# Gate exponentials in one batch, the layer norm on ScalarE in place, and another SyncE order in the setup of a Mamba-times-MoE layer

## The chip, the cores and the metric

The kernel runs on one core of a Trainium2 chip. The metric is the device time of one execution in microseconds (us), lower is better. The time before is the median of three runs. One more execution was recorded by the hardware profiler, and every duration below is from that record, counted from its first instruction.

## The reference

Everything is float32. The input x has 2 sequences of 2048 tokens of 256 channels, 4096 tokens in all. It is normalised, goes through a Mamba mixer with an MLP (s) and through a mixture of experts (g), and the two results are multiplied.

```python
xn = layernorm(x)
s = xn + mamba_mixer(rmsnorm(xn))        # d_inner 512, d_state 16, conv of 4, scan over 2048 steps
s = s + silu(rmsnorm(s) @ mlp_w1.T) @ mlp_w2.T
p = softmax(xn @ gate_w + gate_b)        # 8 experts
pk, ek = top_k(p, 2)
g = silu(sum_k pk * (relu(xn @ w1[ek] + b1[ek]) @ w2[ek] + b2[ek]))
out = x + s * g
```

The mixer's scan is h = h * exp(dt * A) + dt * u * B, y = sum over states of h * C, where dt, B and C come from projections of the convolved input.

## The kernel before, in words

The instructions of each engine run in the order in which the program writes them; nothing is reordered by a planner. A small class `Later` delays some instructions by a number of ticks, and `tick()` advances it; generators such as `front(c)` yield "wait" to ask for a tick. So the order of work between the stages is fixed when the program is built.

The tokens stand in eight blocks of 512 (NBLK), each as four rows-of-128 tiles (J). The kernel has two stages.

**The setup** runs over the blocks. `load_x` brings block b into the buffer with tag `B{b}`. `moments(b)` takes mean and variance on VectorE (DVE). `factors` turns them into scales (a logarithm and an exponential on ScalarE, ACT, and a Newton step on DVE). `norm(b)` writes the doubly normalised rows `xr` on ACT (L254) and transposes them on TensorE (PE, L265) into PSUM. `logits(b)` makes the layer-normed rows `xn` in a buffer of its own, tag `C{b}`: two of the four tiles on DVE (L275), two on ACT (L280). It stores them to DRAM (`xnd`, L284), copies the transposed rows out of PSUM into `xrT[b]`, in the buffer `B{b}` that held x (L288), stores these too (`xrd`), and computes the gate logits with small matmuls (L293) into one PSUM bank, `bank_y`.

Every two blocks (GB) make a group of eight tiles, for which `gate(g)` runs on DVE (L378 to L423): the top two experts of each token, a count of the tokens per expert through two matmuls (L394, L397), and from it the row (`slot`) to which each token goes. `gate(g)` also exponentiates the logits on ACT (L417, L419) and computes the two probabilities from them (L420 to L423). `scatter(g)` then issues 16 indirect DMAs on GpSimd (POOL, L435), each of which writes 128 rows of `xn` to their slots in the DRAM tensor `xs_d`; after each stands a memset of one column named `turn` (L442). Between the groups, `forward(3)` runs three ticks of `front(0)`, the projections and convolution of the first block of the scan.

After the fourth group `tiles_of_experts` (L445 to L504) works out which expert each of 39 tiles of 256 rows belongs to. SyncE (SP) then issues, in this order: the weights of the first expert tile (8 loads of 256 KB, L767 and L774), zeros for the unfilled ends of the tiles (`fill_up`, 8 stores, L510), and the first tile's rows `xs` (`rows()`, L892). SP reads the expert numbers and slots out of SBUF as register values before it issues.

`front(0)` continues: `project_x` writes the scan's B and C for the block to the DRAM tensor `bcd` (L580), and `exp_v` and `log_v` make dt (L598 to L617). They use buffers of the tag `yk`, of which there are two; the tile `zeros` holds one of them in the setup. From the first wait after `project_x` on, `draw` also emits expert work. An expert tile is `transpose` (L799), matmuls with w1 (L809), relu (L909), matmuls with w2 (L821), with the next tile's loads in between. Only when `front(0)` has ended are B and C loaded for all eight pairs of states, each 512 KB broadcast to 128 partitions (`load_bc`, L666), into the buffers `B{g}` and `C{g}`.

**The main loop** has 256 steps (block c, channel group d, pair of states g). A step multiplies by B on DVE (L1260), scans on DVE (L1264), multiplies by C on POOL (L1185), and accumulates on PE (L1157). Beside it `draw` emits the expert tiles, later the MLP tiles, so that PE is kept busy.

Of the kernel before, what the change touches and what calls it, by code (L numbers as in the profile page):

```python
# [22 lines left out]
J = T // P  # L23
# [3 lines left out]
NI = NT // P  # L27
TS = 256
JS = TS // P
# [4 lines left out]
NSLOT = NE * CAP  # L34
GB = 2
GI = GB * T // P
# [13 lines left out]
def kernel(  # L50
# [18 lines left out]
    nc = tc.nc  # L69
# [149 lines left out]

    stat = rows.tile([P, 8, NI], F32, tag="x1", name="stat")  # L220
    mv = stat[:, 0:2, :].rearrange("p a i -> p (a i)").rearrange("p (i a) -> p i a", a=2)
    xns, pts = [], {}

    def moments(b):
        st = hpool.tile([P, J, nc.vector.BN_STATS_DIM], F32, tag="hid", name=f"st{b}")
        for j in range(J):
# [39 lines left out]
        pts[b] = pt  # L266

    def logits(b):
        pool, tag = (bcp, f"B{b}") if b else (rows, "xrT")
        xt = xts[b]  # L270
        xn = bcp.tile([P, J, DM], F32, tag=f"C{b}", name=f"xn{b}")
        for j in range(J):
            i = b * J + j
            if j < 2:
                nc.vector.tensor_scalar(  # L275
                    xn[:, j, :], xt[:, j, :], mv[:, i, 0:1], rstd[:, i : i + 1],
                    ALU.subtract, ALU.mult,
                )
            else:
                nc.scalar.activation(  # L280
                    xn[:, j, :], xt[:, j, :], AF.Identity,
                    scale=rstd[:, i : i + 1], bias=moff[:, i : i + 1],
                )
        nc.sync.dma_start(xnd[b], xn)  # L284
        xns.append(xn)
        xrT[b] = pool.tile([P, KM, T], F32, tag=tag, name=f"xrT{b}")
        for k in range(KM):
            nc.scalar.copy(xrT[b][:, k, :], pts[b][k])  # L288
        if b > 0:
            nc.sync.dma_start(xrd[b], xrT[b])  # L290
        for j in range(J):
            for k in range(KM):
                nc.tensor.matmul(  # L293
                    lgp[:, b * J + j, :], xrT[b][:, k, ts(j, P)], gw_sb[:, k, :],
                    start=(k == 0), stop=(k == KM - 1),
                )


    class Later:
# [63 lines left out]
    halves = [rows.tile([P, 5, GI * NE], F32, tag="ys", name=f"halves{k}") for k in range(2)]  # L363
    scratch = rows.tile([P, JS * DM], F32, tag="x1", name="scratch")
    slots = scratch[:, JS * DM - TOPK * NI :].rearrange("p (k i) -> p k i", k=TOPK)

    def gate(g):
        i = slice(g * GI, (g + 1) * GI)
        sh = [P, GI, NE]
        big = [halves[k][:, n, :] for k in range(2) for n in range(5)]  # L370
        sel = [big[n].rearrange("p (i e) -> p i e", e=NE) for n in range(TOPK)]
        lg, left = (big[n].rearrange("p (i e) -> p i e", e=NE) for n in (2, 3))
        mask, tot_e, ahead = (big[n].rearrange("p (e i) -> p e i", e=NE) for n in (4, 5, 6))
        pr = big[7].rearrange("p (i e) -> p i e", e=NE)
        top = [scratch[:, k * GI : (k + 1) * GI] for k in range(TOPK)]
        first, tot = (scratch[:, k * GI : (k + 1) * GI] for k in range(TOPK, TOPK + 2))
        vec = nc.vector
        vec.tensor_tensor(  # L378
            lg, lgp[:, i, :], unr[:, i].unsqueeze(2).to_broadcast(sh), ALU.mult
        )  # L380
# [12 lines left out]
        flat = [P, NE * GI]  # L393
        nc.tensor.matmul(  # L394
            counts[:, 0, :], all1, mask.rearrange("p e i -> p (e i)"), start=True, stop=True
        )
        nc.tensor.matmul(  # L397
            counts[:, 1, :], earlier, mask.rearrange("p e i -> p (e i)"), start=True, stop=True
        )
        vec.tensor_tensor(pr, lg, top[0].unsqueeze(2).to_broadcast(sh), ALU.subtract)  # L400
        vec.tensor_copy(tot_e, counts[:, 0, :].rearrange("p (e i) -> p e i", e=NE))

        vec.tensor_tensor_scan(
            ahead.rearrange("p e i -> p (e i)"), same.rearrange("p e i -> p (e i)"),
            tot_e.rearrange("p e i -> p (e i)"), 0.0, ALU.mult, ALU.add,
        )
        vec.tensor_sub(tot_e, ahead, tot_e)
        vec.tensor_add(tot_e, tot_e, counts[:, 1, :].rearrange("p (e i) -> p e i", e=NE))
        vec.tensor_tensor(
            tot_e, tot_e, ends[:, 0, :].unsqueeze(2).to_broadcast([P, NE, GI]), ALU.add  # L410
        )
        for k in range(TOPK):
            vec.tensor_mul(sel[k], sel[k], tot_e.rearrange("p e i -> p i e"))  # L413
            vec.tensor_reduce(slots[:, k, i], sel[k], AX.X, ALU.add)
            vec.tensor_copy(slot[:, k, i], slots[:, k, i])
        vec.tensor_add(ends[:, 0, :], ends[:, 0, :], ahead[:, :, GI - 1])
        nc.scalar.activation(pr, pr, AF.Exp)  # L417
        vec.tensor_sub(top[1], top[1], top[0])
        nc.scalar.activation(top[1], top[1], AF.Exp)  # L419
        vec.tensor_reduce(tot, pr, AX.X, ALU.add)  # L420
        vec.tensor_single_scalar(tot, tot, 2.0, ALU.mult)
        vec.reciprocal(prob[:, 0, i], tot)
        vec.tensor_mul(prob[:, 1, i], top[1], prob[:, 0, i])  # L423

    turn = small.tile([P, 1], F32, tag="turn", name="turn", bufs=1)

    def to_slots(ins):

        tc.declare_no_dep(ins, group="to_slots", reason="other rows")
        tc.add_to_no_dep_group("to_slots", ins)  # L430

    def scatter(g):
        for i in range(g * GI, (g + 1) * GI):
            for k in range(TOPK):
                r = nc.gpsimd.indirect_dma_start(  # L435
                    out=xs_d,
                    out_offset=bass.IndirectOffsetOnAxis(ap=slot[:, k, i : i + 1], axis=0),
                    in_=xns[i // J][:, i % J, :],
                    in_offset=None,
                )  # L440
                to_slots(r.ins)
                nc.gpsimd.memset(turn, 0.0)  # L442


    def tiles_of_experts():  # L445
# [214 lines left out]
    def load_bc(c, g, which_ones="BC"):  # L660
        later.free("bcd", c)
        for which in which_ones:
            i = "BC".index(which)
            t = bcp.tile([P, 2, T], F32, tag=f"{which}{g}", name=f"{which}{c}_{g}")
            r = i * DS + 2 * g
            nc.sync.dma_start(  # L666
                t, bcd[c][r : r + 2, :].unsqueeze(0).to_broadcast([P, 2, T])
            )
            bct[c, which, g] = t
# [383 lines left out]
    def tick():  # L1053
        later.now += 1
        later.run()
# [10 lines left out]
        logits(b)  # L1066
    factors(GB, NBLK)
    gate(0)
    scatter(0)
    ffns = [Expert(i) for i in range(NTILE)] + [  # L1070
        Mlp(c, hf) for c in range(NBLK) for hf in range(2)
    ]
# [2 lines left out]
    def forward(ticks):  # L1075

        for got in first:
            if got == "wait":
                tick()
                ticks -= 1  # L1080
                if not ticks:
                    return

    for b in range(GB, NBLK + 1):
        if b < NBLK:
            norm(b)
        if b > GB:
            logits(b - 1)
        if b > GB and b % GB == 0:
            gate(b // GB - 1)  # L1090
            scatter(b // GB - 1)
            forward(3)
    tiles_of_experts()
    xrT[1] = rows.tile([P, KM, T], F32, tag="xrT", name="xrTr1")
    nc.sync.dma_start(xrT[1], xrd[1])
    ffns[0].begin()
# [1 line left out]
        ffns[0].load_w1(h)  # L1098
        ffns[0].load_w2(h)
    fill_up()  # L1100
    for _ in ffns[0].rows():
        pass

    hs, ys, y_n, hts, das, dus = {}, {}, {}, {}, {}, {}

# [113 lines left out]
    for got in first:  # L1219
        if got == "wait":  # L1220
            tick()
            if 0 in bcd:
                draw(HALF)
    tick()
    for which in "BC":
        for g in range(DS // 2):
            load_bc(0, g, which)
    for _ in range(LEAD):
        tick()
        draw(HALF)  # L1230
# [118 lines left out]
```

## Time and profile before

| | us |
|---|---|
| median of 3 runs (lowest to highest) | 1624.94 (1622.39 to 1628.21) |
| the profiled execution, its own time | 1645.22 |
| span of the profiled execution, first to last instruction | 1643.2 |
| PE busy in the span | 1412.1 (86%) |
| DVE busy | 1287.7 (78%) |
| POOL busy | 1130.7 (69%) |
| ACT busy | 863.7 (53%) |
| first, second, third and fourth start of L378 (a gate) | 32.10, 62.66, 92.88, 123.03 |
| end of the last scatter instruction | 150.6 |
| first step of the scan (L1264) | 195.9 |

Busy time is what an engine spends in instructions. A line such as "DVE h L1264" means engine, tile written, line of the program. In a timeline the columns are start, duration, engine, line, operation, what is written and read, how many instructions are merged, and in brackets the idle time of the engine just before with what ended it. "SPq" is a DMA issue of SyncE. The profiled execution is 20.3 us longer than the median of the runs shown.

### The profile page before, as it was taken

The numbers are of one execution on the slowest core, as the hardware profiler recorded it, in microseconds if no ns is written. First come the engines' busy times: TensorE is split into PE (matmuls) and PEld (weight loads), VectorE is DVE, ScalarE is ACT, GpSimd is POOL, SyncE is SP. The second block draws the span as 40 slices with busy tenths as digits, with TensorE's granted clock in tenths as the row PEclk, the third lists the DMA queues.
The fourth block names the chain that finished last, engine by engine and source line by source line (L and its number), as shares of the span: only waits on it lengthen the run. The fifth ranks groups of instructions, "written<-read, shape, count | busy, mean of one in ns | idle before, by whom it ended". The sixth has DMA issues, their size and how long they took to land. (4 is left out here: it accounts for less than half of the span.)

```text
span 1643.2 us, 18570 instructions
## 1 busy us (share of the span) xinstructions
PE 1412.1 (86%) x5278; PEld 989.7 (60%) x5278; DVE 1287.7 (78%) x1452; ACT 863.7 (53%) x1832; POOL 1130.7 (69%) x809
## 2 busy tenths in 40 slices
PE   2543769999899999998999999999889879799967
PEld 2430537677567766675677666756566556567736
DVE  7234457877997899869988998798699978899952
ACT  3421644655566556544765565556645555555513
POOL 1654034667688868986898689868885587878842
PEclk7655879999999999999999999999999989899978
DMA  5444544349244924582358245833582336735322
GB/s 184 152 168 143 210 162 132 100 142 345 65 130 156 325 81 124 154 311 87 111 185 315 77 127 175 296 100 104 189 312 72 103 103 210 259 114 167 115 90 83
DMA packets 203718, 266.22 MB, mean 162 GB/s; under 512 B 21713, under 2 KB 174161, under 8 KB 203617
## 3 DMA queue, kind: packets, MB, share of 16 engines
q1 hardware_dynamic: 197472, 248.26, 45.7%
q0 software_dynamic: 6144, 16.79, 3.1%
q8 instruction: 42, 0.69, 0.2%
q14 instruction: 60, 0.48, 0.1%
HBM read 228.02 MB, written 36.96 MB: 161 GB/s over the span
## 5 line engine op out<-in xcount | busy, mean ns | idle before, releaser
L1185 POOL TENSOR_TENSOR h<-h,C 128x1024 f32<-128x1024 f32 x256 | 609.0, 2381 | 321.5 <-ACT hs L1181 201.2
L1264 DVE TENSOR_TENSOR_SCAN h<-da,hs,b 128x512 f32<-128x512 f32 x384 | 481.3, 1272 | 27.5 <-PE y L1157 4.6
L1144 ACT ACTIVATE da<-dt,a_neg 128x512 f32<-128x512 f32 x512 | 357.2, 718 | 36.9 <-DVE h L1264 36.8
L1157 PE MATMUL y<-h,ident 128*128 128x512 f32 x626 | 315.1, 608 | 24.5 <-POOL h L1187 22.4
L1260 DVE TENSOR_TENSOR b<-du,B 128x1024 f32<-128x1024 f32 x256 | 314.7, 1229 | 7.8 <-DMA B<-bcd 1.9
L809 PE MATMUL phe<-xsTe,w_e 128*128 128x256 f32 x1248 | 292.1, 385 | 9.3 <-ACT hide L909 4.0
L821 PE MATMUL poe<-w_e,hide 128*128 128x256 f32 x1248 | 289.3, 381 | 0.0
L809 PEld LDWEIGHTS phe<-xsTe,w_e 128*128 128x128 f32 x1248 | 239.7, 193 | 78.7 <-issue 29.8
L821 PEld LDWEIGHTS poe<-w_e,hide 128*128 128x128 f32 x1248 | 236.5, 191 | 64.6 <-issue 32.4
L1187 POOL TENSOR_TENSOR h<-h 128x512 f32<-128x512 f32 x199 | 257.9, 1296 | 15.6
L909 ACT ACTIVATE hide<-phe,b 128x256 f32<-128x256 f32 x312 | 129.7, 468 | 143.0 <-PE phe L809 143.0
L1157 PEld LDWEIGHTS y<-h,ident 128*128 128x128 f32 x626 | 116.8, 193 | 117.4 <-issue 66.4
L1264 DVE TENSOR_TENSOR_SCAN h<-da,b 128x512 f32<-128x512 f32 x128 | 152.0, 1212 | 15.3 <-PE y L1157 6.5
L809 PE MATMUL phm<-xsTm,w_m 128*128 128x256 f32 x512 | 125.6, 399 | 22.6 <-DVE hidm L970 17.4
L809 PEld LDWEIGHTS phm<-xsTm,w_m 128*128 128x128 f32 x512 | 101.8, 201 | 51.8 <-DVE hidm L970 20.3
L821 PE MATMUL pom<-w_m,hidm 128*128 128x256 f32 x512 | 122.2, 389 | 2.5 <-DVE xom L1041 1.7
L821 PEld LDWEIGHTS pom<-w_m,hidm 128*128 128x128 f32 x512 | 99.3, 196 | 29.4 <-issue 13.3
L435 POOL DMA_INDIRECT xs_d<-xn,slot x64 | 62.3, 973 | 73.3 <-DVE halves L413 61.9
L997 POOL DMA_INDIRECT ykm<-ys_d,row_y x64 | 61.4, 960 | 36.3 <-issue 12.2
L552 DVE SCALAR_TENSOR_TENSOR xc<-px,par_sb,xc 128x512 f32<-128x512 f32 x96 | 71.6, 746 | 13.0 <-ACT xc L544 10.6
L968 ACT ACTIVATE hidm<-phm 128x512 f32<-128x512 f32 x64 | 37.5, 590 | 77.0 <-PE phm L809 76.6
L921 DVE TENSOR_TENSOR ys<-poe,b 128x512 f32<-128x512 f32 x39 | 26.6, 681 | 50.9 <-PE poe L821 48.6
(175 smaller groups left out, 1433.1 us busy)
## 6 DMA issues: line engine op xcount, KB each, us to landing
w_e<-in_w SPq DMA_DIRECT2D x312, 256.0 KB
B<-bcd SPq DMA_DIRECT2D x64, 512.0 KB
C<-bcd SPq DMA_DIRECT2D x64, 512.0 KB
w_m<-in_mlp_w1T SPq DMA_DIRECT2D x64, 256.0 KB
w_m<-in_mlp_w2T SPq DMA_DIRECT2D x64, 256.0 KB
xs<-xs_d SPq DMA_DIRECT2D x39, 256.0 KB
ys_d<-ys SPq DMA_DIRECT2D x39, 256.0 KB
b<-in_b SPq DMA_DIRECT2D x39, 128.0 KB
```

Of the source, the lines that this page charges most:

```text
L435: r = nc.gpsimd.indirect_dma_start(out=xs_d, out_offset=bass.IndirectOffsetOnAxis(ap=slot[:, k, i : i + 1], axis=0), in_=xns[i // J][:, i ...
L552: nc.vector.scalar_tensor_tensor(v[:, s : s + T], px, conv_w[:, d, KC - 1 - s : KC - s], v[:, s : s + T], ALU.mult, ALU.add,)
L809: nc.tensor.matmul(ph[:, q, :], self.w1[c0 // 2][:, k, ts(q, P)], self.xT[:, k, :], start=(k == 0), stop=(k == KM - 1),)
L821: nc.tensor.matmul(po[:, j, :], self.hid[c // 2][:, c % 2, ts(j, P)], self.w2[c // 2][:, c % 2, :], start=(c == 0 and j == 0), stop=(c == ...
L909: nc.scalar.activation(hc[:, q, :], ph[:, q, :], AF.Relu, bias=self.b1[:, c0 + q : c0 + q + 1])
L997: nc.gpsimd.indirect_dma_start(out=yk[k][:, j, :], out_offset=None, in_=ys_d, in_offset=bass.IndirectOffsetOnAxis(ap=row_y[:, k, i0 + j : ...
L1144: nc.scalar.activation(das[n][:, q, :], dts[c, d], AF.Exp, scale=a_neg[:, d, 2 * g + q : 2 * g + q + 1])
L1157: nc.tensor.matmul(ys[c, d], ident, hts[n][:, q, :], start=False, stop=(g == DS // 2 - 1 and q == nq - 1),)
L1185: nc.gpsimd.tensor_tensor(hts[n], hts[n], bct[c, "C", g], ALU.mult)
L1187: nc.gpsimd.tensor_tensor(hts[n][:, 0, :], hts[n][:, 0, :], hts[n][:, 1, :], ALU.add)
L1260: nc.vector.tensor_tensor(inp, dus[c, d].unsqueeze(1).to_broadcast([P, 2, T]), bct[c, "B", g], ALU.mult,)
L1264: nc.vector.tensor_tensor_scan(hts[n][:, q, :], das[n][:, q, :], inp[:, q, :], 0.0 if c % CPB == 0 else hs[c - 1][:, d, 2 * g + q : 2 * g ...
```

## The change

The exponentials leave the gate. Each `gate(g)` writes its shifted logits into a part of one tile for all groups, `exps_of` (tag `yk`), and the difference of the two top logits into `behind`. A new function `probabilities()`, called once after `tiles_of_experts`, does the two exponentials and the four DVE operations for all 32 tiles together.

The layer norm is done by ACT alone, for all four tiles of a block, in place in the buffer of x, and after the copies and logits matmuls instead of before them. `xrT[b]` goes to the buffer `C{b}`. So `B{b}` is now the buffer from which rows are scattered.

The scatter loses the memset and has a bounds check. `front(0)` gets one tick after every block from the fourth on, six in all, instead of three ticks after every second block, nine in all.

In SP's order the loads of B and C, and the first tile's rows, move: at the first wait after `project_x`, six loads of B, eight of C, the first tile's rows, and the last two of B are issued, ahead of the second tile's weights. The zeros stay behind the first tile's weights.

```diff
     def logits(b):
-        pool, tag = (bcp, f"B{b}") if b else (rows, "xrT")
-        xt = xts[b]
-        xn = bcp.tile([P, J, DM], F32, tag=f"C{b}", name=f"xn{b}")
-        for j in range(J):
-            ...
-            if j < 2:
-                nc.vector.tensor_scalar(xn[:, j, :], xt[:, j, :], mv[...], rstd[...], ...)
-            else:
-                nc.scalar.activation(xn[:, j, :], xt[:, j, :], AF.Identity, ...)
-        nc.sync.dma_start(xnd[b], xn)
-        xns.append(xn)
+        pool, tag = (bcp, f"C{b}") if b else (rows, "xrT")
         xrT[b] = pool.tile([P, KM, T], F32, tag=tag, name=f"xrT{b}")
         ...
+        xn = xts[b]
+        for j in range(J):
+            i = b * J + j
+            nc.scalar.activation(
+                xn[:, j, :], xn[:, j, :], AF.Identity,
+                scale=rstd[:, i : i + 1], bias=moff[:, i : i + 1],
+            )
+        nc.sync.dma_start(xnd[b], xn)
...
+    behind = scratch[:, JS * DM - (TOPK + 1) * NI : JS * DM - TOPK * NI]
+    exps_of = rows.tile([P, NI, NE], F32, tag="yk", name="exps_of")
     def gate(g):
...
-        pr = big[7].rearrange("p (i e) -> p i e", e=NE)
+        pr = exps_of[:, i, :]
...
-        nc.scalar.activation(pr, pr, AF.Exp)
-        vec.tensor_sub(top[1], top[1], top[0])
-        nc.scalar.activation(top[1], top[1], AF.Exp)
-        vec.tensor_reduce(tot, pr, AX.X, ALU.add)
-        vec.tensor_single_scalar(tot, tot, 2.0, ALU.mult)
-        vec.reciprocal(prob[:, 0, i], tot)
-        vec.tensor_mul(prob[:, 1, i], top[1], prob[:, 0, i])
+        vec.tensor_sub(behind[:, i], top[1], top[0])
+
+    def probabilities():
+        nc.scalar.activation(exps_of, exps_of, AF.Exp)
+        nc.scalar.activation(behind, behind, AF.Exp)
+        tot = scratch[:, 0:NI]
+        nc.vector.tensor_reduce(tot, exps_of, AX.X, ALU.add)
+        nc.vector.tensor_single_scalar(tot, tot, 2.0, ALU.mult)
+        nc.vector.reciprocal(prob[:, 0, :], tot)
+        nc.vector.tensor_mul(prob[:, 1, :], behind, prob[:, 0, :])
...
-    def scatter(g):
+    def scatter(i, k):
+        r = nc.gpsimd.indirect_dma_start(
+            out=xs_d,
+            ...
+            in_=xts[i // J][:, i % J, :],
+            in_offset=None,
+            bounds_check=NSLOT - 1,
+            oob_is_err=False,
+        )
+        to_slots(r.ins)
+
+    def scatter_group(g):
         for i in range(g * GI, (g + 1) * GI):
             for k in range(TOPK):
-                r = nc.gpsimd.indirect_dma_start(out=xs_d, ..., in_=xns[i // J][:, i % J, :], in_offset=None)
-                to_slots(r.ins)
-                nc.gpsimd.memset(turn, 0.0)
+                scatter(i, k)
...
             gate(b // GB - 1)
-            scatter(b // GB - 1)
-            forward(3)
+            scatter_group(b // GB - 1)
+        if b > GB:
+            forward(1)
     tiles_of_experts()
+    probabilities()
...
     fill_up()
-    for _ in ffns[0].rows():
-        pass
...
     for got in first:
         if got == "wait":
             tick()
-            if 0 in bcd:
+            if 0 in bcd and not bct:
+                last = DS // 2 - GB
+                for g in range(last):
+                    load_bc(0, g, "B")
+                for g in range(DS // 2):
+                    load_bc(0, g, "C")
+                for _ in ffns[0].rows():
+                    pass
+                for g in range(last, DS // 2):
+                    load_bc(0, g, "B")
+            if bct:
                 draw(HALF)
-    tick()
-    for which in "BC":
-        for g in range(DS // 2):
-            load_bc(0, g, which)
```

More of the change, by code (lines that the diff above doesn't have):

```diff
@@ L221 @@
     mv = stat[:, 0:2, :].rearrange("p a i -> p (a i)").rearrange("p (i a) -> p i a", a=2)
-    xns, pts = [], {}
+    pts = {}
     def moments(b):
@@ L268, in logits @@
     def logits(b):
-        pool, tag = (bcp, f"B{b}") if b else (rows, "xrT")
-        xt = xts[b]
-        xn = bcp.tile([P, J, DM], F32, tag=f"C{b}", name=f"xn{b}")
-        for j in range(J):
-            i = b * J + j
-            if j < 2:
[L275 to L278, printed above, removed]
-            else:
[L280 to L283, printed above, removed]
-        nc.sync.dma_start(xnd[b], xn)
-        xns.append(xn)
+        pool, tag = (bcp, f"C{b}") if b else (rows, "xrT")
         xrT[b] = pool.tile([P, KM, T], F32, tag=tag, name=f"xrT{b}")
@@ L373, in gate @@
         mask, tot_e, ahead = (big[n].rearrange("p (e i) -> p e i", e=NE) for n in (4, 5, 6))
-        pr = big[7].rearrange("p (i e) -> p i e", e=NE)
+        pr = exps_of[:, i, :]
         top = [scratch[:, k * GI : (k + 1) * GI] for k in range(TOPK)]
-        first, tot = (scratch[:, k * GI : (k + 1) * GI] for k in range(TOPK, TOPK + 2))
+        first = scratch[:, TOPK * GI : (TOPK + 1) * GI]
         vec = nc.vector
@@ L416, in gate @@
         vec.tensor_add(ends[:, 0, :], ends[:, 0, :], ahead[:, :, GI - 1])
-        nc.scalar.activation(pr, pr, AF.Exp)
-        vec.tensor_sub(top[1], top[1], top[0])
-        nc.scalar.activation(top[1], top[1], AF.Exp)
-        vec.tensor_reduce(tot, pr, AX.X, ALU.add)
-        vec.tensor_single_scalar(tot, tot, 2.0, ALU.mult)
-        vec.reciprocal(prob[:, 0, i], tot)
-        vec.tensor_mul(prob[:, 1, i], top[1], prob[:, 0, i])
-    turn = small.tile([P, 1], F32, tag="turn", name="turn", bufs=1)
+        vec.tensor_sub(behind[:, i], top[1], top[0])
[7 more added lines that the diff above has]
+        nc.vector.tensor_mul(prob[:, 1, :], behind, prob[:, 0, :])
     def to_slots(ins):
@@ L430, in to_slots @@
         tc.add_to_no_dep_group("to_slots", ins)
-    def scatter(g):
+    def scatter(i, k):
+        r = nc.gpsimd.indirect_dma_start(
+            out=xs_d,
+            out_offset=bass.IndirectOffsetOnAxis(ap=slot[:, k, i : i + 1], axis=0),
+            in_=xts[i // J][:, i % J, :],
[5 more added lines that the diff above has]
+    def scatter_group(g):
         for i in range(g * GI, (g + 1) * GI):
             for k in range(TOPK):
[L435 to L440, printed above, removed]
-                to_slots(r.ins)
-                nc.gpsimd.memset(turn, 0.0)
+                scatter(i, k)
     def tiles_of_experts():
@@ L1068 @@
     gate(0)
-    scatter(0)
+    scatter_group(0)
     ffns = [Expert(i) for i in range(NTILE)] + [
```

## Prediction

> **What bounds the kernel now.** First the rows of 40 slices (41 us each), which show where an engine stands idle.
>
> ```profile
> span 1643.2 us, 18570 instructions
> ...
> PE   2543769999899999998999999999889879799967
> ...
> POOL 1654034667688868986898689868885587878842
> ```
>
> From the seventh slice on TensorE is 80 to 100% busy almost to the end: the main loop is bound by TensorE, and the change alters no instruction of it. The first five and a half, to about 220 us, are half empty. Whatever the change does, it does there, and the loop then follows as a block. So I price the point at which TensorE begins to flow, the start of the third expert tile's transposes (L799, 215.16 us).
>
> Next the waits of the first 232 us, engine by engine (engine, line, who ended the wait: total us, times, longest).
>
> ```profile
> DVE halves L378 <- remote: 51.9, 3, 20.5
> ...
> POOL xs_d L435 <- DVE halves L413: 61.9, 4, 31.9
> ...
> ACT halves L417 <- DVE halves L400: 49.3, 4, 16.0
> ...
> ACT xrT L288 <- DVE stat L233: 7.1, 1, 7.1
> ...
> PE pxse L799 <- DMA xs<-xs_d: 32.7, 2, 20.6
> ```
>
> Two chains stand here. The first is gate, scatter, gate, scatter: POOL waits for a gate's slots, ScalarE's exponential L417 waits for the gate, and everything behind L417 in ScalarE's order (the next blocks' norms) waits too. The second is SyncE's order: TensorE waits for rows of an expert tile. The timeline gives both.
>
> ```profile
> 49.96 3.64 PE L293 MATMUL bank_y<-gw_sb,xrT 128*128 128x8 f32 x16 [0.83 <-ACT xn L280]
> ...
> 59.86 0.11 POOL L442 MEMSET turn<- 128x1 f32 x1
> 62.66 0.23 DVE L378 TENSOR_TENSOR halves<-bank_y,unr 128x64 f32<-128x64 f32 x1 [20.45 <-remote]
> ...
> 69.86 0.96 POOL L435 DMA_INDIRECT xs_d<-xn,slot  x1 [9.88 <-DVE halves L413]
> ...
> 155.91 8.73 SPq L510 DMA_DIRECT2D xs_d<-zeros  x8
> 166.48 0.40 SPq L892 DMA_DIRECT2D xs<-xs_d  x1
> ...
> 194.56 9.84 SPq L666 DMA_DIRECT2D C<-bcd  x8
> ...
> 206.70 0.40 SPq L892 DMA_DIRECT2D xs<-xs_d  x1
> ...
> 215.16 1.08 PE L799 MATMUL pxse<-ident,xs 128*128 128x128 f32 x4 [12.19 <-DMA xs<-xs_d]
> ```
>
> In the first half the second gate needs only TensorE's logits L293, which end at 53.60. It starts at 62.66, 2.7 us after POOL's last scatter instruction. The third and fourth gates do the same (87.48 and 92.88; 116.56 and 123.03): **9.1, 5.4 and 6.5 us late, 20.9 together**. The profiled execution took 1645.22 us, 20.3 above the median of 1624.94. I choose the reading that the timed runs do not have this late release; the other reading is a rival below. In the second half B and C (16 loads) come after two tiles' weights, the third tile's rows are behind them, and TensorE idles 12.2 us.
>
> **What the Trainium skill says.** "Perfetto Trace Analysis", DMA Instruction — SWDGE (GPSIMD): the profile's end of such a DMA is when its descriptors are written, not when data has landed. The trace agrees: the scatter at 39.59 lasts 1.24 us, its semaphore rises at 42.09. "SBUF — State Buffer", Who interferes with whom: a VectorE tensor_scalar in a two-port mode can block GpSimd. The trace shows none: beside the four L275 at 40.83 to 42.21 the scatter takes 0.97 us, as elsewhere, so taking L275 from VectorE gives POOL nothing. "DMA: Bandwidth & Descriptors", Two DMAs through the same engine are not ordered: within one queue descriptors start in order. The trace agrees: rows issued at 206.70, behind the last C load, reach TensorE at 215.16.
>
> **The change, part by part.** All against the profiled times less the late releases, which puts the fourth gate of before at 123.03 - 20.9 = 102.1, the last scatter's end at 150.6 - 20.9 = 129.7, the last zeros issue at 164.6 - 20.9 = 143.7.
>
> *Norm on ScalarE in x's place, xrT in C.* VectorE loses four L275 ahead of the first gate (1.35 us). ScalarE's copy L288 of block 1 no longer waits 7.1 us for them, so it is not in front of the logarithm L213 (about 0.9). The first gate starts at 32.1 - 2.2 = 29.9, the first scatter at 39.6 - 2.2 = 37.4. ScalarE gains 16 activations of 0.54 us, 8.6 us over some 120 in which it is under 40% busy; I count them in the chain below.
>
> *Exponentials at the end.* L417, L419 and L420 to L423 leave the gate. Nothing on the way from gate to scatter needs them (L435 starts before L420), but ScalarE is free at 30 instead of 40.2. Second gate: norms of blocks 2 and 3 to 34, gate's counts on TensorE at 34 to 35, transposes to 39, copies and in-place norm to 40, first tick's px and widening to 44, norm of block 4 to 46, copies to 47, L293 to 50.5. Its slots are ready at 58, when POOL has just ended the first group: 37.4 + 16 x 1.27 = 57.7. By the same steps the third gate starts near 71 and the fourth near 89, each with slots at or ahead of POOL. **POOL then runs all 64 scatters nearly without a gap: 37.4 + 64 x 1.27 + 0.5 = 119.2, against 129.7: 10.5 us earlier.** The probabilities add about 1 us to VectorE after the tiles of experts and the later silu another 4; both end near 116, long before SyncE is free for bcd, so I cost them at nothing. If SyncE were faster, 5 us would appear.
>
> *The scatters.* The memset is gone, a bounds check is new. Nearest row without memset, the gather:
>
> ```profile
> L997 POOL DMA_INDIRECT ykm<-ys_d,row_y x64 | 61.4, 960 | 36.3 <-issue 12.2
> ```
>
> Back to back, gathers start 1.26 us apart, scatters with memset 1.27: the memset is worth 0.01 x 64 = 0.6. No page and no row prices the check. Below: it cannot remove work, and a shorter scatter would soon wait for gates, so at most 4 us gained. Above: I estimate a third of the 0.96 us, 0.3 x 64 = 19. I take zero.
>
> *SyncE.* While scatters run, weight issues come 2.8 us apart (143.00, 145.82, 148.65, 151.50); after 152.9 the rest and eight zeros need 11.8 us. With the scatters' end moved 10.5 us and one weight more issued before it (0.6), the last zeros issue is at 143.7 - 11 = 132.7.
>
> *B and C ahead.* Before, from the last zeros: rows wait 1.7 us for zeros, land at 169.4, 4.8 us after; TensorE works to 203.0 (33.6 us), idles 12.2, and starts the third tile 50.5 us after the last zeros. After: bcd 0.4, landing 2.5 (the scatter's above), then 14 loads of 512 KB at the 387 GB/s seen from 195 to 220: 7.34 MB, 19.0 us; rows 1.5, half of the 3.0 between issue and L799 of the first rows before, as the queue is already moving. The first rows land 23.4 us after the zeros. The same 33.6 us of tiles follow, less 1.4, since ScalarE's table load (169.67) is past by then. The third tile has no wait left: 55.6. **So this part costs 5.1 us**: the idle time is moved ahead of the first tile, not removed. Queued behind it are the last two B (used at step 6), the second tile's weights (needed 21 us later) and, on TensorE and ScalarE, everything behind the first transposes. ScalarE's first ex now also waits for the zeros, since exps_of holds the other yk buffer: two sets of 3.2 us, done 10 us before the rows. Covered.
>
> Sum: -11 + 5.1 = **-5.9 us**. Against the profile that alone is 1639.3; against the median, which lacks the late releases by my choice, 1624.9 - 5.9 = **1619.0**.
>
> **Rivals.**
> - *The late release is real in timed runs, before and after.* For it: it is in the record three times. Against: the 20.3 us between profile and median. Then gates wait for scatters again, the fourth starts near 121.7, zeros end 1.4 us earlier and the load order costs 5.1: +3.7, 1628.6.
> - *The late release is real before and ends with the memsets.* Then before is not shortened: scatters end 31 us earlier, minus 5.1: 1599. Only the coincidence of places (it appears only beside scatters) speaks for it.
> - *Slower: the bounds check lengthens each scatter on POOL.* POOL is the chain with no slack after the change, so each 0.1 us costs 6.4. From 0.09 us a scatter it eats the gain; at 0.3 the sum is +13, 1638. For it: POOL's 0.96 us are work per row, and a check is work per row. Against: nothing measured.
> - *The change does less than it says*: first rows late anyway because scatters end late. No: rows would wait to 122, and they are queued to 155.
>
> **How the numbers follow.** Forecast 0.42, spread 1611 to 1626; real in both 0.20; ended by the memsets 0.08; bounds check 0.30. Over 0.3% (4.9 us, about what a measurement of this kernel can tell from none) faster: 0.36 of the forecast's and the 0.08, 0.44. Within: 0.06 and 0.15 of the second, 0.21. Slower: 0.05 and 0.30, 0.35. The range leaves out the ended-by-memsets end and the top of the check: 1604 to 1640. The forecast's own is 1611 to 1626.
>
> **What would show it.** Right: no ScalarE exponential inside gates; scatter groups of POOL without gaps between them (apart from a late release in the profile); B and C issued straight after bcd, TensorE idle some 20 us before its first L799 and not before its third. Wrong: scatters further than 1.35 us apart (bounds check); gates later than 51, 71, 89 in the absence of a late release; a third L799 that still waits for rows; main-loop slices that differ.

## The result and the profile after

On the chip of the forecast's own comparison the changed kernel takes 1616.0 us (median of 20 runs), the kernel before 1622.88 (20 runs): a ratio of 0.9952, 95% interval 0.9936 to 0.9968, or 5 to 10 us less. Forecast were 1619.0 and 5.9 us less. The profiled execution of the changed kernel took 1621.06 us.

The rows of 40 slices (40.5 us each) of the changed kernel, TensorE and GpSimd:

```profile
span 1619.4 us, 18570 instructions
...
PE   3753899999999999989999999999888978899967
...
POOL 1770234686789768966997689668985687878842
```

TensorE is full from the sixth slice, at 200 us, where it was the seventh. POOL's second and third slices, the scatters, are 7 where they were 6 and 5: the same 64 scatters with less between them. The rest is the old loop, earlier.

The waits of its first 232 us (engine, line, who ended the wait: total us, times, longest), and its timeline:

```profile
DVE halves L372 <- PE bank_y L276: 31.6, 3, 14.7
...
POOL xs_d L428 <- ACT xrT L271: 30.7, 2, 30.4
...
ACT ex L597 <- DMA xs_d<-zeros: 4.8, 1, 4.8
...
PE pxse L798 <- DMA xs<-xs_d: 28.2, 1, 28.2
...
SPq L878 <- DVE scratch L490: 13.7, 1, 13.7
```

```profile
52.67 0.22 DVE L372 TENSOR_TENSOR halves<-bank_y,unr 128x64 f32<-128x64 f32 x1 [14.69 <-PE bank_y L276]
60.42 0.97 POOL L428 DMA_INDIRECT xs_d<-xt,slot  x1 [1.85 <-issue]
73.12 0.23 DVE L372 TENSOR_TENSOR halves<-bank_y,unr 128x64 f32<-128x64 f32 x1 [10.46 <-PE bank_y L276]
90.13 0.22 DVE L372 TENSOR_TENSOR halves<-bank_y,unr 128x64 f32<-128x64 f32 x1 [6.47 <-PE bank_y L276]
...
113.42 9.63 SPq L509 DMA_DIRECT2D xs_d<-zeros  x8
...
126.87 3.57 SPq L665 DMA_DIRECT2D B<-bcd  x6
130.49 7.46 SPq L665 DMA_DIRECT2D C<-bcd  x8
138.98 0.40 SPq L891 DMA_DIRECT2D xs<-xs_d  x1
140.23 1.59 SPq L665 DMA_DIRECT2D B<-bcd  x2
...
148.47 1.12 PE L798 MATMUL pxse<-ident,xs 128*128 128x128 f32 x4 [28.24 <-DMA xs<-xs_d]
```

The gate is L372 now. Each of the three later gates starts the moment TensorE has its logits (L276) ready, in the middle of a scatter group; "remote" (the profile names no instruction that ended the wait) and the late release are gone. POOL has one gap of 1.85 us in 64 scatters. ScalarE's second ex waits 4.8 us for the zeros, done long before the first rows; the first ex, of which the forecast expected this, does not wait for them. B and C go out ahead of the first rows, and TensorE stands 28.24 us before its first expert tile and not at all before its third.

So the profiled executions differ by 24.2 us (1645.22 and 1621.06) and the timed runs by 7. Where the other 17 are is the main question below.

The groups of instructions by line, for the disputed bounds check (busy us, mean ns):

```profile
L428 POOL DMA_INDIRECT xs_d<-xt,slot x64 | 62.6, 978 | 51.2 <-ACT xrT L271 30.7
```

978 ns a scatter, starts 1.28 us apart. The unchanged scatter has 974 ns and 1.27 us (from the profile of the kernel that is called "scatters moved" below).

### The profile page after: what moved, and what is told of

Its sections match the earlier page's. It is cut to its first block, busy times and chain, and to the rows that moved or that the text cites. A ratio compares the mean times of both kernels' runs of the same rounds, so it can differ in the third digit from the quotient of the medians.

```text
span 1619.4 us, 18570 instructions
## 1 busy us (share of the span) xinstructions
PE 1422.2 (88%) x5278; PEld 995.5 (61%) x5278; DVE 1280.0 (79%) x1424; ACT 870.5 (54%) x1842; POOL 1122.7 (69%) x745
## 5 line engine op out<-in xcount | busy, mean ns | idle before, releaser
L1156 PE MATMUL y<-h,ident 128*128 128x512 f32 x626 | 318.0, 612 | 24.8 <-POOL h L1186 21.2
L808 PE MATMUL phe<-xsTe,w_e 128*128 128x256 f32 x1248 | 297.9, 391 | 7.8 <-ACT hide L908 4.0
L808 PEld LDWEIGHTS phe<-xsTe,w_e 128*128 128x128 f32 x1248 | 244.1, 196 | 79.4 <-issue 30.3
L808 PEld LDWEIGHTS phm<-xsTm,w_m 128*128 128x128 f32 x512 | 103.2, 203 | 52.6 <-DVE hidm L969 20.3
L428 POOL DMA_INDIRECT xs_d<-xt,slot x64 | 62.6, 978 | 51.2 <-ACT xrT L271 30.7
```

Of the source, the lines that this page charges most:

```text
L428: r = nc.gpsimd.indirect_dma_start(out=xs_d, out_offset=bass.IndirectOffsetOnAxis(ap=slot[:, k, i : i + 1], axis=0), in_=xts[i // J][:, i ...
L808: nc.tensor.matmul(ph[:, q, :], self.w1[c0 // 2][:, k, ts(q, P)], self.xT[:, k, :], start=(k == 0), stop=(k == KM - 1),)
L1156: nc.tensor.matmul(ys[c, d], ident, hts[n][:, q, :], start=False, stop=(g == DS // 2 - 1 and q == nq - 1),)
```

## The experiments

They ran as three sets, each on one chip, with the kernel before run beside them. On the first two chips the kernel before takes 1652.18 and 1651.35 us; on the third it takes 1624.64, as on the chip of the forecast's comparison. I call the first two kind B and the last two kind A. Only comparisons within a set are used for ratios.

### First set, kind B

**The kernel before, unchanged**, for a second profile.

> The kernel before, unchanged, profiled once more. Theory A (late release of the gates belongs to that one profiled execution): L378 starts when the logits matmuls end, near 32, 54, 78 and 102 us, and the profiled execution takes 1620 to 1630 us. Theory B (the late release is part of every execution): L378 again starts near 62.7, 92.9 and 123.0, about 2.8 us after the last scatter of the group, and the profiled execution takes about 1645 us.

1654.64 us. The waits of VectorE in its first 225 us:

```profile
DVE halves L378 <- remote: 51.0, 3, 20.3
```

The gates start at 32.02, 62.45, 92.58 and 122.70, each of the last three 2.7 to 3.0 us after the end of a scatter group, and the first four weights are issued 2.1 to 3.5 us apart. This is the profile on which the forecast was made, over again. And its own time is only 2.5 us above this chip's median: here the timed runs look like the profile.

**Only the scatters' edit**, on the kernel before.

```diff
                 r = nc.gpsimd.indirect_dma_start(
                     ...
                     in_offset=None,
+                    bounds_check=NSLOT - 1,
+                    oob_is_err=False,
                 )
                 to_slots(r.ins)
-                nc.gpsimd.memset(turn, 0.0)
```

> The kernel before with the scatter of after alone (no memset, bounds check). Theory A (the gain comes from ScalarE being free of the gates): same as before within 2 us; scatters 1.27 us apart. Theory B (the memsets or the missing check hold the gates up): faster than before by most of the 7.8 us. Slower rival of the prediction: more than 6 us slower, scatters over 1.35 us apart.

1651.42 us, ratio 1.0001 (0.9982 to 1.002). Starts are 1.28 us apart instead of 1.27; the three gates are late as before (62.69, 92.90, 123.01). The bounds check costs what the memset cost, and the memsets do not hold the gates: two rivals fall here.

**Only the load order**, on the kernel before: the last part of the change's diff.

```diff
     fill_up()
-    for _ in ffns[0].rows():
-        pass
     ...
-            if 0 in bcd:
+            if 0 in bcd and not bct:
+                last = DS // 2 - GB
+                for g in range(last):
+                    load_bc(0, g, "B")
+                for g in range(DS // 2):
+                    load_bc(0, g, "C")
+                for _ in ffns[0].rows():
+                    pass
+                for g in range(last, DS // 2):
+                    load_bc(0, g, "B")
+            if bct:
                 draw(HALF)
-    tick()
-    for which in "BC":
-        for g in range(DS // 2):
-            load_bc(0, g, which)
```

> The kernel before with SyncE's load order of after alone. Theory A: 5 us slower than before, since TensorE then idles some 20 us for the first tile's rows instead of 12 us for the third tile's. Theory C (the load order is what gains): 8 us faster than before.

1656.64 us, ratio 1.0021 (1.0009 to 1.0032): 3.5 us slower by the ratio, where 5 were expected. Its waits of TensorE in the first 225 us:

```profile
PE pxse L799 <- DMA xs<-xs_d: 39.6, 1, 39.6
```

One wait of 39.6 us where the kernel before (profile of this set) has two of 33.6 in all. The idle time is moved ahead of the first tile, and grows.

**Everything but the load order**: the changed kernel with that diff undone.

> The kernel after with SyncE's load order of before. Theory A: 12 to 13 us faster than before (5 us faster than after), the first rows right after the zeros. Theory C: no faster than before.

1646.27 us, ratio 0.9963 (0.9949 to 0.9976): 6 us faster than the kernel before, half of what was expected. In its profile two of the three later gates still wait for a group's end (60.97 and 91.41, 2.4 and 2.6 us after it). The last one starts in mid group (112.66), but 4.1 us after TensorE's logits ended. This execution is the slowest of its 22, 6.7 us above their median, so the typical one may lose less.

### Second set, kind B

**The changed kernel again.**

> The changed kernel as it is, for its own time beside the kernel before on this chip, and for a second profile. If the two parts run alone add up (load order alone +3.5 us, everything but the load order -6 us): -2.5 us. As forecast, and as on the first chip: -6 to -8 us. If what the first profile of the changed kernel showed, gates that never wait for the scatters, is what timed runs have here: -24 to -31 us.

1648.8 us, ratio 0.9983 (0.997 to 0.9996): 2.5 us less. The two parts alone gave -0.37% and +0.21%; together they give -0.17%: they add up. The later gates are at 56.59, 86.89 and 105.84, which is 7.5, 9.8 and 1.9 us after the logits ended. The fourth is 17 us ahead of the kernel before's on this kind of chip, and yet the expert numbers reach SyncE at 139.5, as they did there (138.5). The timeline of VectorE shows where it went:

```profile
123.39 0.31 DVE L458 TENSOR_SCALAR scratch<-scratch 128x8 f32<-128x8 f32 x1 [3.22 <-remote]
124.79 0.29 DVE L461 TENSOR_TENSOR over<-scratch,steps 128x128 f32<-128x128 f32 x1 [1.09 <-DVE scratch L458]
126.19 0.29 DVE L465 TENSOR_REDUCE scratch<-over 128x8 f32<-128x128 f32 x1 [1.11 <-DVE over L461]
```

These are three steps of `tiles_of_experts`, each of which waits for VectorE's own step before. They start 1.40 us apart. In the third set's profile of the same program they start 0.2 and 0.33 us apart:

```profile
97.54 0.17 DVE L458 TENSOR_SCALAR scratch<-scratch 128x8 f32<-128x8 f32 x1
97.74 0.29 DVE L461 TENSOR_TENSOR over<-scratch,steps 128x128 f32<-128x128 f32 x1
98.07 0.29 DVE L465 TENSOR_REDUCE scratch<-over 128x8 f32<-128x128 f32 x1
```

Between two such steps stands a semaphore (a counter that one instruction raises at its end and the next waits for). The trace records when it changes: L458 ends at 123.70, the change is recorded at 124.77, and L461 starts 0.02 us after that; on kind A the same change is recorded 0.01 us after L458 has ended. From L455 to the end of L483 the chain takes 19.0 us on kind B and 4.1 on kind A, though POOL scatters beside them in both. So on kind B a semaphore that should rise while scatters run rises late, VectorE's own as well as the one that a gate waits for: every later gate in the nine profiles of kind B starts 0.6 to 10.2 us after its logits ended, and every one in the five of kind A 0.04 us after. (The weights, 2.1 to 3.5 us apart beside scatters, may have the same cause; that was not followed.)

It is not late from the first scatter on: in the kernel before on kind B the same VectorE chain lies 4.3 to 8.5 us into the fourth group and takes 4.2 us. The logits of the gates, all late, end 9.3 us or more after the first scatter of an unbroken run.

In the changed kernel the third and fourth groups follow without a gap (94.58 to 135.24), and the chain begins 25 us into that stretch. **So the 17 us that this execution gains at the fourth gate are gone where SyncE waits for the expert numbers.** The scatters end earlier all the same, the weights follow 0.6 us apart after them, and the last zeros are issued at 155.5 instead of 164.2: 8.7 us of gain are left there. But this execution is 7.5 us faster than the median of its runs, so the typical gain on kind B is less, and which part of it the typical run lacks was not seen.

**The first tile's rows ahead of B and C**, on the changed kernel.

```diff
     fill_up()
+    for _ in ffns[0].rows():
+        pass
     ...
                 for g in range(DS // 2):
                     load_bc(0, g, "C")
-                for _ in ffns[0].rows():
-                    pass
```

> The changed kernel with the first tile's rows issued straight after the zeros, then B and C, then the second tile's weights. If the cost of the load order lies in the first tile waiting 25.8 us behind B and C: the first L798 about 4 us after the last zeros instead of 25.8, the third 15 to 19 us earlier than in the changed kernel, and the time 12 to 19 us below it. If the idle time of TensorE only moves to the second or third tile: within 3 us of it.

1638.35 us, ratio 0.993 (0.9905 to 0.9955): 13 us below the kernel before, 10.5 below the changed one, a little less than expected. The first L798 is 5.1 us after the last zeros, the third 47.1 after them (in the changed kernel of this set 23.8 and 56.5).

**Exponentials and probabilities back in each gate**, on the changed kernel.

```diff
+        nc.scalar.activation(pr, pr, AF.Exp)
         vec.tensor_sub(behind[:, i], top[1], top[0])
+        nc.scalar.activation(behind[:, i], behind[:, i], AF.Exp)
+        ...
     tiles_of_experts()
-    probabilities()
```

> The changed kernel with the exponentials and the probabilities back at the end of each gate. If the gain comes from ScalarE, which stands at a gate's exponential instead of norming the next blocks: second to fourth gates 5 to 8 us later each, gaps of some 7 us between the scatter groups, the time 6 to 10 us above the changed kernel. If the gates are held by something else: within 2 us of it.

1652.36 us, ratio to the kernel before 1.0009 (0.9995 to 1.0023); 3.6 us above the changed kernel by medians, less than the 6 to 10 expected. ScalarE's waits in its first 232 us show what the edit does:

```profile
ACT exps_of L411 <- DVE exps_of L394: 38.0, 4, 12.6
```

Four times, 38 us in all, ScalarE stands at a gate's exponential, with the next blocks' norms behind it. The changed kernel of this set stands there once, for 5.6 us, at the one exponential of `probabilities`. All three later gates are late (60.81, 91.15, 121.51, each 2.4 to 2.5 after a group's end).

**The layer norm as before**, on the changed kernel: half of it on VectorE, into a buffer of its own, ahead of the copies (the first hunk of the change undone).

> The changed kernel with the layer norm as before: half on VectorE, into a buffer of its own, ahead of the copies. By the forecast's step the first gate and first scatter are 2.2 us later and the scatters still run without gaps: 2 us above the changed kernel. If the 16 activations that ScalarE gained were what holds the gates: 2 to 5 us below it.

1653.5 us, ratio to the kernel before 1.001 (0.9999 to 1.0022); 4.7 above the changed kernel by medians, where 2 were expected. The first gate is 2.2 us later (32.16), as the forecast's step had it, the first scatter 1.6 us (39.64). But there is more to the edit, as ScalarE's waits show:

```profile
ACT xrT L287 <- DVE xn L274: 35.4, 3, 16.5
```

ScalarE's copies follow VectorE's half of the norm, and VectorE stands in a gate, waiting for TensorE. I had not seen this wait in the forecast: with the norm on ScalarE alone the copies no longer wait behind a gate. Either edit undone brings all later gates back to the groups' ends on kind B; the two losses, 3.6 and 4.7, are more than the 6 us that the two bring together with the scatters' edit. They are not separate gains.

### Third set, kind A

**Scatters moved**: in the program of the kernel before, all 64 scatters are written after the fourth gate.

```diff
     gate(0)
-    scatter(0)
     ...
             gate(b // GB - 1)
-            scatter(b // GB - 1)
             forward(3)
+    for g in range(NBLK // GB):
+        scatter(g)
     tiles_of_experts()
```

> The kernel before with all 64 scatters after the fourth gate, so that no gate stands beside a scatter. If the late release of gates is in timed runs on this chip, the kernel before pays it (fourth gate 123, last scatter 150.6) and this one does not: gates near 32, 51, 70, 90, scatters from 98 to 179, first rows 15 us later than before, time +12 to +18 us. If timed runs have no late release, the kernel before's last scatter is at 129.7 in them and this one's still at 179: +33 to +39 us, unless the wait of rows hides some of it, then at least +25.

1623.82 us, ratio 0.9995 (0.9979 to 1.001). Both expectations failed, since the edit does nothing: POOL has no other work between the scatters, and a scatter waits for its slots only, so the first is at 39.59 as ever. It is therefore no test of the late release. But it gives what was missing, a profile of the kernel before's setup on kind A. (The last kernel of this set, whose setup is the unaltered one, has the same gates within 0.06 us.) Its waits in the first 232 us, and its timeline:

```profile
DVE halves L378 <- PE bank_y L293: 31.9, 3, 12.4
...
SPq L879 <- DVE scratch L490: 19.8, 1, 19.8
```

```profile
54.60 0.22 DVE L378 TENSOR_TENSOR halves<-bank_y,unr 128x64 f32<-128x64 f32 x1 [12.39 <-PE bank_y L293]
79.96 0.23 DVE L378 TENSOR_TENSOR halves<-bank_y,unr 128x64 f32<-128x64 f32 x1 [12.35 <-PE bank_y L293]
87.16 0.96 POOL L435 DMA_INDIRECT xs_d<-xn,slot  x1 [5.25 <-DVE halves L413]
103.69 0.23 DVE L378 TENSOR_TENSOR halves<-bank_y,unr 128x64 f32<-128x64 f32 x1 [7.17 <-PE bank_y L293]
...
121.65 0.39 SPq L767 DMA_DIRECT2D w_e<-in_w  x1
122.23 0.38 SPq L774 DMA_DIRECT2D w_e<-in_w  x1
...
127.43 9.24 SPq L510 DMA_DIRECT2D xs_d<-zeros  x8
139.49 0.40 SPq L892 DMA_DIRECT2D xs<-xs_d  x1
...
142.39 1.12 PE L799 MATMUL pxse<-ident,xs 128*128 128x128 f32 x4 [12.78 <-DMA xs<-xs_d]
189.74 1.09 PE L799 MATMUL pxse<-ident,xs 128*128 128x128 f32 x4 [13.76 <-DMA xs<-xs_d]
```

No gate waits for "remote". The third tile starts at 189.74; on kind B (first set) it starts at 220.21, 30.5 us later, of which 27.9 are there at the last zeros (164.2 and 136.3). From the third tile to the end both take the same within 2.6 us. The chips differ by 26.7 us in timed runs (1651.35 less 1624.64). So the difference of the chips lies in this setup, and, as far as these profiles stand for the timed runs, those of kind B have the late release and those of kind A do not.

**The changed kernel once more.**

> The changed kernel once more, for a third profile and a third comparison. On a chip where the kernel before takes about 1651: -2.5 us and one to three of the second to fourth gates released late. On a chip where it takes about 1623: -7.8 us and none late.

1613.61 us, ratio 0.9944 (0.9924 to 0.9964), none of the gates late: as expected on kind A, a little better. Its timeline:

```profile
86.83 0.22 DVE L372 TENSOR_TENSOR halves<-bank_y,unr 128x64 f32<-128x64 f32 x1 [6.63 <-PE bank_y L276]
...
109.59 9.39 SPq L509 DMA_DIRECT2D xs_d<-zeros  x8
...
119.32 0.97 POOL L428 DMA_INDIRECT xs_d<-xt,slot  x1 [0.30 <-issue]
...
143.82 1.12 PE L798 MATMUL pxse<-ident,xs 128*128 128x128 f32 x4 [27.35 <-DMA xs<-xs_d]
164.21 0.60 PE L798 MATMUL pxse<-ident,xs 128*128 128x128 f32 x4
180.18 0.60 PE L798 MATMUL pxse<-ident,xs 128*128 128x128 f32 x4
```

**The first tile's rows ahead of B and C, once more**, and **the same order of loads on the kernel before** (its own place for the rows kept, B and C ahead of the second tile's weights):

```diff
-            if 0 in bcd:
+            if 0 in bcd and not bct:
+                last = DS // 2 - GB
+                for g in range(last):
+                    load_bc(0, g, "B")
+                for g in range(DS // 2):
+                    load_bc(0, g, "C")
+                for g in range(last, DS // 2):
+                    load_bc(0, g, "B")
+            if bct:
                 draw(HALF)
-    tick()
-    for which in "BC":
-        ...
```

> The changed kernel with the first tile's rows ahead of B and C, once more. As measured: -13 us against the kernel before, -10.5 against the changed kernel. If the first figure was the chance of how many gates were late in its runs: within 5 us of the changed kernel.

> The kernel before, first tile's rows as before straight after the zeros, B and C then ahead of the second tile's weights: only this part of the load order. If the forecast's cost of the load order is all in the first tile's rows: the third tile's L799 about 47 us after the last zeros instead of 56, time -7 to -10 us. If loads of B and C ahead of the second tile's weights cost by themselves: 0 or above.

The first takes 1597.76 us (four runs only), ratio 0.9829 (0.9795 to 0.9862): 22 to 33 us below the kernel before and some 16 below the changed one by medians, more than expected. The profiled execution is the slowest of the four (1608.74), 5.4 us below the changed kernel's, so the size is uncertain. Its timeline:

```profile
127.20 0.40 SPq L891 DMA_DIRECT2D xs<-xs_d  x1
130.05 1.11 PE L798 MATMUL pxse<-ident,xs 128*128 128x128 f32 x4 [8.14 <-DMA xs<-xs_d]
130.36 3.41 SPq L665 DMA_DIRECT2D B<-bcd  x6
...
155.10 0.66 PE L798 MATMUL pxse<-ident,xs 128*128 128x128 f32 x4 [2.76 <-DMA xs<-xs_d]
...
172.81 0.60 PE L798 MATMUL pxse<-ident,xs 128*128 128x128 f32 x4
```

TensorE works on the first tile while B and C land. The third tile starts 48.8 us after the last zeros (issued at 124.0), where the changed kernel needs 61.6. This version beats both kernels on both kinds of chip.

The second takes 1617.25 us, ratio 0.9961 (0.9946 to 0.9975): 6 us faster, where 7 to 10 were expected. The third tile starts 49.5 us after the last zeros, instead of 53.4: B and C ahead of further weights gains by itself; only the first rows behind them cost.

## Why the prediction was right, and where not

The two profiles of one kind of chip (A: scatters moved, and the changed kernel once more) give each step its size. Zeros are counted here, as in the experiments, to the start of the last one's issue; the forecast counted to its end, 0.4 us later, and its figures are put in this count.

| us | before | after | difference | forecast |
|---|---|---|---|---|
| fourth gate starts | 103.69 | 86.83 | -16.9 | -13 (102.1, 89) |
| last scatter ends | 131.28 | 120.29 | -11.0 | -10.5 (129.7, 119.2) |
| last zeros issued | 136.3 | 118.6 | -17.7 | -11 (143.3, 132.3) |
| third tile after them | 53.4 | 61.6 | +8.1 | +5.1 (50.9, 56.0) |
| the last two together, third tile starts | 189.74 | 180.18 | -9.6 | -5.9 |

**The reading that was chosen, timed runs without the late release: right for the times shown**, and it decided the forecast. The five profiles of kind A show no late gate, and the kernel before's last scatter there ends 1.6 us from where the forecast put it by subtraction. That the 20.9 us of late gates so nearly equalled the 20.3 us between profile and median was in part chance: at the last zeros kind A is 28.0 us ahead of that profile, and the profile's own time is 6 to 7 us below the medians of kind B. The reading is wrong on kind B, where the release is in timed runs. The profiled execution of before belongs to kind B by its records: traces of kind B hold 18,885 to 19,016 records of semaphore changes, those of kind A 20,568 to 20,642, for nearly the same work; the one that the forecast read holds 18,939. The profile and the times beside it were not of one kind, and this is the 20.3 us that separated them. It is also where the 17 us go that the two profiled executions differ by beyond the timed runs: before was profiled as on kind B, after as on kind A.

**Rival "real in both"** is what kind B does, with gates late in both kernels. It said +3.7; measured is -2.5. Its sum took over the load order's +5.1, which is +3.5 there, and had every later gate wait for a group's end, while in three profiles of kernels with the change's gates one or two of them are released before it, 0.6 to 7.5 us after their logits.

**Norm and exponentials: right.** First gate 29.9 to 30.0, as forecast; later gates forecast at 51, 71, 89, measured 49.15, 69.65, 86.83 in one execution and 52.67, 73.12, 90.13 in another. POOL's waits for later gates, 10.7 us in all in the kernel before on kind A, are at most 1.85. The first scatter is 0.7 us later than forecast (38.1). The probabilities cost nothing that shows. Left out was the copies' wait behind VectorE's gate.

**Scatter: right.** Nothing within 0.01 us each.

**SyncE: the step that failed.** The forecast took the late release out of the profile and left in the slow weights beside scatters, 2.8 us apart. Both are seen on kind B only. On kind A weights are issued 0.6 us apart while POOL scatters (121.65, 122.23 above). Then SyncE does not follow the scatters' end at all: it waits 19.8 us for the expert numbers (L879 on L490), which follow the fourth gate. From that gate to the last zeros are 32.6 us before and 31.8 after. So the fourth gate's 16.9 us were the right term, not the scatters' 11: 6.7 us too little.

**B and C ahead: right; TensorE's clock is the rest of the +8.1.** The first tile starts 25.2 us after the zeros (forecast 23.8 in this count), and the third then has no wait, as said. But the two tiles between take 36.4 us, not 32.2. The 20 us from the first tile's start show why. The columns are the stretch and its length, the busy time of TensorE, its loads, VectorE, ScalarE and GpSimd, then the granted clock of TensorE (1.00 is full), DMA share and GB/s. The changed kernel on kind A (third set) and on kind B (second set):

```profile
143.82:163.82 20.00, 19.32 (x55) 13.50 (x56) 2.82 (x5) 11.01 (x21) 0.00 (x0) 0.65 0.37 120
```

```profile
179.31:199.31 20.00, 19.32 (x74) 14.60 (x75) 4.06 (x6) 11.39 (x22) 0.00 (x0) 0.84 0.45 145
```

The kernel before on kind A (scatters moved) and on kind B (first set):

```profile
142.39:162.39 20.00, 17.86 (x70) 13.72 (x71) 7.43 (x11) 13.98 (x26) 0.00 (x0) 0.85 0.36 112
```

```profile
169.33:189.33 20.00, 17.89 (x48) 12.25 (x49) 4.75 (x7) 13.07 (x25) 0.00 (x0) 0.61 0.27 85
```

In the same busy time the same program does 55 matmuls at a granted clock of 0.65 and 74 at 0.84. Of the 14 profiles seven have 0.60 to 0.66 here and seven 0.82 to 0.87, with each of the two programs, and each kind of chip, on both sides. So the clock goes neither with the change nor with the chip. The length of the idle time ahead of the tile does not decide it either: 27.35 us went before the 0.65, 24.8 before the 0.84, and 8.14 before the 0.60 of the changed kernel with the rows ahead.

With the change's load order the two tiles take 32.2 to 32.7 us in the three profiles with the higher clock, as forecast, and 36.1 to 36.4 in the three with the lower. The Trainium skill ("TensorE: Matmul & The Clock Gate", Part 1) has the clock rise only after a window of about 3.4 us of sustained work, and windows that run freely, so that the time at the low clock varies from run to run. The traces agree that it varies, but not in size: after the tile's start the clock stays at half for 5.1 to 7.1 us in seven of them and for 13.6 to 16.2 us in the other seven. Why there are two lengths stays open.

The table sets a kernel before at the higher clock against a changed one at the lower. Between executions of like clock this part costs 2.6 to 5.8 us at the third tile, against 5.1 forecast and 3.5 in the timed runs of the load order alone.

The two differences, -6.7 (SyncE) and +3.0, leave -9.6 at the third tile against -5.9. The spans of the two profiles differ by 7.2, so that 2.4 of it do not reach the end; single executions differ by as much. The ratio of the timed runs, 0.9944, is 9 us; on the forecast's chip it was 8. **So the number is nearer than its terms, and that is in part luck.** With like clocks, the 17.7 us at the zeros less 2.6 to 5.8 would be, as an estimate, 12 to 15 us at the third tile. What takes the rest of it from the timed runs, the lower clock in more of them or a gain that is lost in the main loop, was not measured.

**Left open.** Why semaphores rise late beside scatters on some chips, and whether the missing records are its cause or a sign of it. That the kind goes with the chip is the simplest reading of a few sets, not more. No kernel took the scatters away from beside the gates; the one that was meant to did not. The exponentials and the norm were put back on kind B alone, so on kind A their shares of the 16.9 us at the fourth gate are not known.

## What to carry to other kernels

Before pricing a part, compare the profiled execution's own time with the times: where they are apart by more than the spread of the runs, the profile shows another condition, and everything that it causes must be taken out together, not only the symptom that was noticed. The same holds for the profile of an experiment: some of those here are 7 us or more to one side of the median of their runs. Find what an issuing queue really waits for before tying it to the nearest busy engine: on kind A SyncE hung on the fourth gate, not on the scatters that ended about then. When loads are moved ahead, let the one that starts the bound engine go first, and the bulk behind it.

## What was not expected of the hardware

- With indirect scatters running 1.27 us apart, dependent steps of VectorE start 1.40 us apart on one chip and 0.2 to 0.33 on another, in the same program, as the semaphore between them is recorded 1.07 us after the step's end on the one and 0.01 on the other. In the four traces of kind B in which such a chain lies 4.3 to 8.5 us into a group of scatters, it is not slowed.
- The whole kernel takes 1651 to 1652 us on some chips and 1623 to 1625 on others, and the difference is made in the first 220 us.
- TensorE's granted clock over the first 20 us of expert tiles was 0.60 to 0.66 in seven profiles and 0.82 to 0.87 in seven, the same program on both sides; the length of the idle time before did not decide it.
- An indirect scatter of 128 rows with a bounds check has 978 ns, without it 974.
